# Attention in pairs of units with energies of 512 queries, and two turns moved from TensorE to DRAM blocks

## The chip, the cores and the metric

The kernel runs on one core of a Trainium2 chip. The metric is the device time of one execution in microseconds (us). Short names of the engines: PE is TensorE (its matrix multiplications; PEld its weight loads), DVE is VectorE, ACT is ScalarE, POOL is GpSimd, SP is SyncE, which here only issues transfers (DMAs).

## The reference, cut to what matters

The input `x` has shape (4, 64, 64, 256): four images of 4096 positions with 256 channels. Two layers follow each other.

```python
# layer 0: self-attention over the 4096 positions of an image
q, k, v = x @ wq + bq, x @ wk + bk, x @ wv + bv        # q, k: 32 channels, v: 256
attention = softmax(einsum('bnd,bmd->bnm', q, k))       # 4096 x 4096 per image
y = gamma * einsum('bnm,bmc->bnc', attention, v) + x
# layer 1: deformable convolution (16 groups, 3 x 3 points), then an MLP
h = ln(y) * ln1_g + ln1_b
p = h @ inproj_w                                         # the image that is sampled
t = gelu(ln(depthwise3x3(h)))                            # gives offsets and masks
offset, mask = t @ off_w, softmax(t @ mask_w)
z = y + (sum over points of mask * bilinear(p, point + offset)) @ outproj_w
out = z + gelu((ln(z) * ln2_g + ln2_b) @ fc1_w) @ fc2_w  # 256 -> 1024 -> 256
```

## The kernel before, in words

The work is cut into 64 units of 256 positions (16 per image; `NU` is 16, `UN` is 64). Each unit goes through the same stages, and the stages of neighbouring units overlap:

- `project` computes keys, queries and values. For the first image this is done at the start; for the others one unit at a time beside the attention of the image before. The later images read `x` by `in_blocks` (L70): four DMAs of 64 KB in pieces of 128 bytes that put every 32 x 32 block at its turned place, and one DVE `transpose` (L645) turns inside the blocks.
- `Attention` (the class at L696): for a unit, 32 tiles of 128 keys. `energies` makes 8 key tiles by 256 queries per step (L752, in a single-pass format, fp32r), into four PSUM tiles; `exponentials` lets ACT take the exponential (L762); `weighted` multiplies by the values (L774, plain f32, 257 columns: 256 channels and the row sum) into two accumulators. Every unit loads all keys again (`keys`, L713, two DMAs per 1024 keys).
- `front` scales by the reciprocal of the row sum (L797) and by gamma (L799), adds the input (L803), normalizes, turns on PE and projects (`pp`, L831) into the DRAM image `xp`.
- `plan` does the depthwise convolution on DVE (`cv`, L878), turns, normalizes, makes offsets and masks (`po`, L915), and builds the 5 x 5 weights `wn` of every position. `sums` (L961) and `mask` (L996) are issued once per tile of 128 positions, twice per unit.
- `sample` multiplies windows of 5 x 256 channels (`win`, loaded by two DMAs for each row pair, L1074) by `wn` and adds up, on DVE (`pw`, L1094 and L1102, 1280 elements each). The result `sp` goes to DRAM too (`spd`).
- `back` turns `sp` by four PE transposes (`pt_s`, L331), ACT copies it out of PSUM (L1169), `pout` (L1175) projects, `x1b` is added and normalized, `xn_b` is turned by four PE transposes (`pt_b`), ACT scales it (`hT_b`, L311), `ph` (L1200) and `pmlp` (L1217) are the MLP, and the result is written.

Every instruction of PE, DVE, ACT and POOL stands in an order written out by hand: `WHEN` gives each step of a stage a time in a slot of `T` = 60 (one unit), `LATE` has other times for the last units, and `whole` sorts all steps by these times. The times only order the steps; each engine runs its list in order and waits where something is not there yet. SP issues its DMAs in program order, and a DMA that waits holds up those behind it.

PSUM is full: two rotating tiles `m` for all small products, four tiles for the energies, two accumulators.

Of the kernel before, what the change touches and what calls it, by code (L numbers as in the profile page):

```python
# [20 lines left out]
def tile_attention_dcnv3_block(  # L21
# [126 lines left out]
    gamma_s = bcast(gamma, 1, "gamma_s")  # L148
# [118 lines left out]
    qd = dram.tile([UN, 2, CQ, 256], F32, name="qd")  # L267
# [9 lines left out]
    nc.vector.memset(most_, 1.0)  # L277

# [28 lines left out]
    def scaled(pt, g, b, name, m=256):  # L307

        hT = p3.tile([P, C // P, 256], F32, tag="cT", name=f"hT_{name}")
        for k in range(C // P):  # L310
            nc.scalar.activation(  # L311
                hT[:, k, :m], pt[:, k, :m], AF.Identity, bias=b[:, k : k + 1], scale=g[:, k : k + 1]
            )
        return hT
# [11 lines left out]
    def transposed(src, name, n=2, pool=None, tag="m"):  # L326

        pt = (pool or ps).tile([P, C // P, 256], F32, tag=tag, name=f"pt_{name}")
        for k in range(C // P):
            for i in range(n):  # L330
# [7 lines left out]
    T = 60.0  # L338
    WHEN = {
        "first": {  # L340
# [3 lines left out]
        "project": {  # L344
            "load": -14.4, "turn": 19.72, "copy": 23.24, "values": 37.05, "value_bias": 42.74, "keys": 48.45,
            "key_bias": 50.49,
        },
        "attention": {
            "load": -9.55, "e0": -5.06, "x0": -4.74, "e1": -0.37, "w0": 7.43, "w3": 19.94, "w2": 29.41,
            "x1": 34.36, "w1": 39.1, "w5": 39.21, "e2": 40.0, "w7": 40.03, "x2": 44.45, "w9": 44.91,  # L350
            "e3": 47.79, "w11": 48.15, "w8": 48.54, "w6": 48.74, "x3": 51.26, "w10": 52.64, "w14": 52.81,
            "w13": 56.88, "w4": 57.18, "w12": 58.34, "w15": 58.47,
        },
        "general": {
            "e0": -0.41, "x0": -0.39,
        },
        "tables": {
            "gelu0": -12.71, "gelu1": 13.84, "exp": 41.13,
        },
        "front": {  # L360
            "inverse": -0.5, "residual": -0.39, "stats": -0.12, "shift": 9.44, "norm": 19.11, "keep": 28.97,
            "turn": 29.19, "scale": 30.3, "project_in": 34.83, "image": 34.95, "store": 36.13,
        },
        "plan": {
            "tap0": 36.3, "tap1": 38.26, "tap2": 39.85, "tap3": 40.19, "tap4": 40.72, "tap5": 41.32,
            "tap6": 42.03, "tap7": 42.69, "tap8": 43.18, "turn": 45.14, "stats": 46.03, "shift": 47.25,
            "norm": 48.66, "turn2": 48.72, "gelu": 48.77, "heads0": 49.72, "bias0": 50.5, "heads1": 50.74,
            "bias1": 51.52, "mask_exp": 51.76, "hat0": 52.32, "sums": 52.79, "invert": 53.35, "hat2": 53.4,
            "hat1": 53.43, "weigh": 54.05, "nearer": 56.15, "near": 56.63, "bounds": 56.75, "mask0": 57.34,
            "mask1": 57.68, "product0": 58.16, "y_copies0": 58.81, "y0": 59.03, "product1": 59.29,  # L370
            "y1": 59.54, "y_copies1": 59.55, "carry": 60.61, "x_copies": 60.68, "x": 67.54, "count": 72.45,
        },
        "sample": {
            "rows01": 8.69, "times01": 8.71, "rows00": 19.04, "times00": 19.06, "rows02": 20.69,
            "times02": 20.71, "plus01": 21.46, "plus02": 30.61, "rows03": 31.73, "times03": 31.75,
            "rows04": 34.48, "times04": 34.5, "plus03": 34.93, "plus04": 38.23, "across00": 41.05,
            "across01": 43.53, "rows12": 45.24, "times12": 45.26, "across02": 45.73, "rows11": 45.98,
            "times11": 46.0, "rows10": 46.62, "times10": 46.64, "plus11": 47.22, "plus12": 47.46,
            "rows13": 48.74, "times13": 48.76, "rows14": 49.16, "times14": 49.18, "plus13": 50.33,
            "plus14": 51.1, "across10": 51.57, "across11": 51.74, "across12": 53.08,  # L380
        },
        "back": {
            "load": 18.32, "turn": 54.71, "copy": 54.86, "project_out": 56.05, "added": 58.14, "stats": 58.62,
            "shift": 59.05, "norm": 59.26, "raised": 59.37, "turn2": 59.4, "scale": 59.75, "hidden0": 59.78,
            "hidden5": 61.44, "gelu0": 65.24, "gelu5": 67.65, "hidden1": 68.95, "gelu1": 70.18,
            "hidden2": 73.18, "gelu2": 77.76, "hidden4": 81.06, "gelu4": 84.59, "hidden6": 84.61,
            "hidden7": 87.12, "gelu6": 87.36, "gelu7": 93.93, "hidden3": 99.62, "gelu3": 101.35,
            "narrowed0": 102.2, "narrowed1": 106.29, "end": 106.65,
        },
        "far": {  # L390
            "pair": -84, "point": -80, "left": -77, "rows": -76, "pixels": -74, "summed": -66, "turn": 46.75,
            "copy": 47.03, "project_out": 47.31, "added": 47.59, "stats": 47.87, "shift": 48.15,
            "norm": 48.43, "turn2": 48.72, "scale": 49.0, "raised": 49.28, "hidden0": 49.56, "gelu0": 49.84,
            "hidden1": 50.12, "gelu1": 50.4, "hidden2": 50.68, "gelu2": 50.96, "hidden3": 51.24,
            "gelu3": 51.52, "hidden4": 51.8, "gelu4": 52.08, "hidden5": 52.36, "gelu5": 52.65,
            "hidden6": 52.93, "gelu6": 53.21, "hidden7": 53.49, "gelu7": 53.77, "narrowed0": 54.05,
            "end": 54.33,
        },
        "checks": {
            "range": 14.0, "left": 14.1, "largest": 14.2,  # L400
        },
        "summing": {
            "rows01": 8.69, "times01": 8.71, "rows02": 12.39, "times02": 12.41, "pair01": 16.11,
            "sum01": 19.82, "rows03": 23.5, "times03": 23.52, "rows00": 27.2, "times00": 27.22,
            "sum00": 30.92, "rows04": 34.6, "times04": 34.62, "pair03": 38.33, "sum03": 42.03,
            "rows11": 45.24, "times11": 45.26, "summed0": 45.73, "rows12": 46.02, "times12": 46.04,
            "pair11": 46.82, "sum11": 47.61, "rows13": 48.37, "times13": 48.39, "rows10": 49.15,
            "times10": 49.17, "sum10": 49.95, "rows14": 50.71, "times14": 50.73, "pair13": 51.52,
            "sum13": 52.3, "summed1": 53.08,
# [5 lines left out]
        "attention": {  # L415
            60: {"e2": 41.63, "w7": 60.7, "x2": 61.55, "e3": 66.3, "w11": 68.16, "w10": 72.05, "x3": 77.04,
                "w4": 92.63, "w12": 96.73, "w14": 126.44, "w13": 147.54, "w6": 149.16, "w9": 151.58,
                "w8": 162.58, "w15": 163.18},
            61: {"load": 73.15, "e0": 77.73, "x0": 99.75, "e1": 104.68, "w0": 119.31, "x1": 120.96,
                "w4": 128.82, "w7": 135.45, "e2": 139.75, "w5": 140.73, "x2": 142.59, "w6": 144.13,  # L420
                "w9": 144.35, "e3": 145.78, "w11": 147.04, "w10": 148.04, "x3": 148.67, "w3": 150.79,
                "w13": 152.23, "w14": 153.3, "w2": 155.04, "w1": 159.09, "w12": 159.2, "w8": 161.6,
                "w15": 162.84},
            62: {"load": 99.58, "e0": 109.75, "x0": 110.1, "e1": 115.56, "w0": 118.27, "w2": 120.32,
                "x1": 120.74, "w6": 125.15, "e2": 126.82, "w5": 128.98, "x2": 130.87, "w7": 131.07,
                "e3": 132.81, "w11": 137.28, "w10": 140.15, "w1": 141.18, "x3": 141.21, "w3": 142.52,
                "w14": 145.25, "w4": 147.03, "w13": 147.58, "w12": 147.88, "w8": 148.09, "w9": 149.05,
                "w15": 151.71},
            63: {"load": 96.28, "e0": 109.66, "x0": 111.02, "w0": 116.5, "w1": 120.49, "e1": 121.69,
                "x1": 130.68, "w4": 132.65, "w5": 134.09, "e2": 139.76, "w2": 143.15, "w3": 145.56,  # L430
                "w6": 148.75, "x2": 149.1, "w10": 151.15, "e3": 151.17, "w7": 152.54, "w8": 159.2,
                "x3": 160.16, "w14": 161.32, "w12": 166.1, "w9": 172.0, "w13": 173.2, "w11": 173.78,
                "w15": 178.59},
        },
        "plan": {
            60: {"tap3": 42.14, "tap4": 45.5, "tap5": 45.93, "tap6": 48.85, "tap7": 56.79, "tap8": 69.29,
                "turn": 71.67, "stats": 84.78, "shift": 119.53, "norm": 125.14, "turn2": 134.12,
                "gelu": 136.3, "heads0": 139.79, "heads1": 139.85, "bias0": 140.11, "bias1": 141.55,
                "hat0": 143.63, "hat2": 145.22, "mask_exp": 149.39, "hat1": 152.25, "sums": 155.5,
# [170 lines left out]
                "summed0": 541.21},  # L610
        },
        "checks": {
            66: {"range": 530.02, "left": 563.34, "largest": 1080.93},
        },
    }

# [921 lines left out]
```

## Time and profile before

| | |
|---|---|
| time, median of 3 runs | 3755.57 us (3753.74 to 3757.58) |
| the profiled execution: time, span | 3755.45 us, 3753.7 us |
| PE busy | 3693.6 us (98%) |
| DVE busy | 3442.1 us (92%) |
| ACT busy, with 380 loads of a function table of 1283 ns | 2122.0 us (57%) |
| DMA, mean busy share of the 16 engines of queue q1 | 51.9%, 508 MB |
| mean granted PE clock | 0.995 |

The span reaches from the first instruction to the last; the other 1.75 us of the profiled execution lie around it. Busy time counts an engine once where its instructions overlap. Since they do overlap on PE and DVE, the mean duration of an instruction is longer than the distance between the starts of two in a dense row; this distance is called the pitch below, and sums of work are made with it. A page line of part 5 has the line, engine, operation, output and inputs, shape and count, then busy time and mean duration, then the idle time ahead of the group and what ended it.

### The profile page before, as it was taken

The page shows a single profiled execution, that of the slowest core. Times are in us where ns is not written, and L with a number is a line of the kernel's source. Part 1 is how long each engine was busy: PE and PEld are TensorE (multiplying, and loading weights), DVE is VectorE, ACT ScalarE, POOL GpSimd, SP SyncE. Part 2 cuts the span into 40 slices and gives each one's busy share as a digit, 9 for nine tenths or more (in the row PEclk, how much of TensorE's full clock was granted, in tenths as well). Part 3 has the DMA queues.
Part 4 walks back from the last instruction along what each step waited for, and adds up shares of the span by engine and source line. Part 5 has one row for each costly group of instructions (what it writes and reads, how often), then busy time and mean ns, then how long its engine had stood idle before and what let it go on. Part 6 is the DMA issues. An engine that isn't in the chain of part 4 may idle for free.

```text
span 3753.7 us, 53218 instructions
## 1 busy us (share of the span) xinstructions
PE 3693.6 (98%) x18226; PEld 3185.1 (85%) x18226; DVE 3442.1 (92%) x6307; ACT 2122.0 (57%) x4085; POOL 313.1 (8%) x444
## 2 busy tenths in 40 slices
PE   7999999999999999999999999999999999999988
PEld 6888888888888888888888888888888888888867
DVE  2499999999999999999999999999999999999995
ACT  2465565565565565565565555555565665565543
POOL 1000000000000000000000000000000000000021
PEclk9999999999999999999999999999999999999999
DMA  6555545556555555555656455555565545544531
GB/s 185 142 130 140 143 129 140 141 129 175 149 149 146 138 131 143 134 135 143 176 137 164 129 138 142 129 139 140 138 174 146 136 124 136 132 129 126 135 83 52
DMA packets 370088, 518.42 MB, mean 138 GB/s; under 512 B 144560, under 2 KB 287472, under 8 KB 369808
## 3 DMA queue, kind: packets, MB, share of 16 engines
q1 hardware_dynamic: 359904, 508.02, 51.9%
q10 hardware_dynamic: 8320, 3.43, 0.4%
q8 instruction: 147, 2.41, 0.3%
q0 software_dynamic: 1584, 3.47, 0.3%
q14 instruction: 133, 1.09, 0.1%
HBM read 385.91 MB, written 128.85 MB: 137 GB/s over the span
## 4 chain that ended last, share of the span: by engine, by line
PE 89%; DVE 5%; issue 0%; DMA 0%; ACT 0%; POOL 0%; DVEq 0%; SPq 0%; ACTq 0%; POOLq 0%
PE acc L774 43%; PE pmlp L1217 11%; PE ph L1200 11%; PE e L752 6%; PE po L915 5%; PE pout L1175 3%; PE pp L831 3%; PE pv L670 2%; DVE pw L1094 1%; PE pkq L651 1%; DVE cv L878 1%; DVE pw L1102 1%; PE pt_s L331 1%; PE pt_b L331 1%; PE pt_p L331 1%; PE pc L891 1%
## 5 line engine op out<-in xcount | busy, mean ns | idle before, releaser
L774 PE MATMUL acc<-V,ex 128*128 128x257 f32 x8192 | 1887.0, 380 | 0.0
L774 PEld LDWEIGHTS acc<-V,ex 128*128 128x128 f32 x8192 | 1537.3, 190 | 223.3 <-issue 21.7
L1094 DVE TENSOR_TENSOR pw<-win,wn 128x1280 f32<-128x1280 f32 x640 | 931.5, 1481 | 10.9 <-ACT wn L1038 1.9
L1102 DVE TENSOR_TENSOR pw<-pw,pw 128x1280 f32<-128x1280 f32 x492 | 729.7, 1483 | 0.1
L762 ACT ACTIVATE ex<-e 128x512 f32<-128x512 f32 x1024 | 529.7, 605 | 26.1 <-PE e L752 18.0
L1200 PE MATMUL ph<-hT_b,f1w 128*128 128x256 f32 (+1 forms) x2080 | 487.9, 377 | 5.2 <-ACT gT L1208 2.8
L1217 PE MATMUL pmlp<-f2w,gT 128*128 128x256 f32 x2048 | 462.7, 379 | 1.3 <-DVE x1b L1182 1.1
L1200 PEld LDWEIGHTS ph<-hT_b,f1w 128*128 128x128 f32 x2080 | 378.1, 190 | 67.3 <-ACT gT L1208 6.3
L1217 PEld LDWEIGHTS pmlp<-f2w,gT 128*128 128x128 f32 x2048 | 384.2, 190 | 51.8 <-DVE x1b L1182 1.4
L878 DVE SCALAR_TENSOR_TENSOR cv<-hs,dw,cv 128x256 f32<-128x256 f32 (+1 forms) x1076 | 424.3, 459 | 1.4 <-ACT cv L874 1.3
L303 ACT ACTIVATE xn_p<-pc,nm_p,rstd_p 128x256 f32<-128x256 f32 x128 | 65.4, 561 | 541.1 <-DVE nm_p L295 541.1
L1208 ACT ACTIVATE gT<-ph,f1b 128x256 f32<-128x256 f32 (+1 forms) x520 | 236.6, 468 | 236.1 <-PE ph L1200 234.6
L752 PE MATMUL e<-qs,kT 128*128 128x256 f32 x2048 | 321.7, 300 | 0.0
L752 PEld LDWEIGHTS e<-qs,kT 128*128 128x128 f32 x2048 | 271.4, 190 | 8.1 <-ACT ex L762 0.8
L762 ACT ACT_TABLE_LOAD x182 | 233.5, 1283 | 3.1
L289 POOL TENSOR_SCALAR rstd_p<-mv_p 128x2 f32<-128x2 f32 (+1 forms) x65 | 76.2, 1172 | 1669.1 <-DVE mv_p L287 1597.9
L915 PE MATMUL po<-om_w,ge 128*128 128x432 f32 x512 | 196.5, 526 | 0.8 <-ACT ge L908 0.8
L1004 DVE TENSOR_TENSOR pr<-hat 128x1296 f32<-128x1296 f32 x128 | 192.6, 1505 | 0.0
L1208 ACT ACT_TABLE_LOAD x124 | 159.1, 1283 | 2.2
L915 PEld LDWEIGHTS po<-om_w,ge 128*128 128x128 f32 x512 | 96.9, 190 | 70.5 <-issue 54.7
L908 ACT ACTIVATE ge<-pt_p,bd,gd 128x256 f32<-128x256 f32 (+1 forms) x130 | 66.0, 558 | 137.9 <-PE pt_p L331 137.9
L303 ACT ACTIVATE xn_b<-x1b,nm_b,rstd_b 128x256 f32<-128x256 f32 x128 | 70.0, 593 | 129.8 <-DVE nm_b L295 129.8
(220 smaller groups left out, 3823.0 us busy)
## 6 DMA issues: line engine op xcount, KB each, us to landing
win<-xp SPq DMA_DIRECT2D x536, 320.0 KB, 4.5
kT<-kd SPq DMA_DIRECT2D x512, 256.0 KB, 4.2
omd<-om SPq DMA_DIRECT2D x63, 432.0 KB, 2.6
x<-in_x_dram SPq DMA_DIRECT2D x64, 256.0 KB, 3.0
x1d<-x SPq DMA_DIRECT2D x64, 256.0 KB, 2.2
xp<-xq SPq DMA_DIRECT2D x128, 128.0 KB, 2.4
x1b<-x1d SPq DMA_DIRECT2D x63, 256.0 KB, 3.2
spd<-sp SPq DMA_DIRECT2D x63, 256.0 KB, 2.2
```

Of the source, the lines that this page charges most:

```text
L303: nc.scalar.activation(xn[:, i, :], s, AF.Identity, bias=nm[:, i : i + 1], scale=st["r"][:, i : i + 1])
L752: nc.tensor.matmul(es[r][:, jj, :], lhsT=self.kT[g][:, 4 * jj + r, :], rhs=self.qs.bitcast(F32R), start=True, stop=not self.general,)
L762: nc.scalar.activation(ex, self.es[r], AF.Exp)
L774: nc.tensor.matmul(self.acc[i], lhsT=ex[:, jj, i * P : (i + 1) * P], rhs=V[t // 2][:, t % 2, :], start=(g == 0 and r == 0 and jj == 0), st ...
L878: nc.vector.scalar_tensor_tensor(dst, src, dw[:, k, j : j + 1], dst, ALU.mult, ALU.add)
L915: nc.tensor.matmul(st["po", i], lhsT=st["ge"][:, k, i * P : (i + 1) * P], rhs=om_w[:, k, :], start=(k == 0), stop=(k == 1),)
L1004: nc.vector.tensor_mul(pr.rearrange("p a b c d g -> p a b (c d g)"), hat[:, :, i, 1, :].unsqueeze(1).to_broadcast([P, 3, 3, S]), hat[:, :, ...
L1094: nc.vector.tensor_mul(st[r].rearrange("p d (g c) -> p (d g) c", c=GC), src.rearrange("p d (g c) -> p (d g) c", c=GC), wns[v][:, i, r] .re ...
L1102: nc.vector.tensor_add(st[0], st[0], st[r])
L1200: nc.tensor.matmul(ph[:, :m], lhsT=f1w[:, k, c * P : (c + 1) * P], rhs=st["hT"][:, k, :m], start=(k == 0), stop=(k == 1),)
L1208: nc.scalar.activation(st["gT"][:, c, :m], st["ph", c][:, :m], AF.Gelu, bias=f1b[:, c : c + 1])
L1217: nc.tensor.matmul(po, lhsT=st["gT"][:, c, i * P : (i + 1) * P], rhs=f2w[:, c, :], start=(c == 0), stop=(c == NH - 1),)
```

## The change

The change has four parts.

1. Attention works on pairs of units. A slot is now a pair (`T` = 120). `energies(j)` makes 2 key tiles by 512 queries; 16 such steps per pair. It needs two PSUM tiles instead of four; each accumulator becomes a two-bank tile that holds both halves of one unit. `weighted(u, j)` is the same work as before, for one unit of the pair. The keys are loaded once per pair, by one DMA per 1024 keys, and the queries by two DMAs per pair. The last two units (62 and 63) run alone, with 256 queries, as before.
2. In `back` of units 1 to 58, `sp` and `xn_b` are not turned by PE. `sp` is read back from `spd` by `in_blocks` (four DMAs) and turned in its blocks by a DVE transpose into `sT`, so ACT's copy goes. `xn_b` is written to a small DRAM tile (`ways`), read back by four DMAs, turned by a DVE transpose (`swap`), and scaled by ACT in place. Both, and the input of `project`, use one tile, tag `xs`, of which there is one buffer.
3. DVE: gamma is multiplied into the value weights once, so L799 goes (128 instructions); one reciprocal per unit in place of two; `sums` and `mask` once per unit in place of twice.
4. `win` of a row pair is loaded by one DMA in place of two. All times of `WHEN` and `LATE` are new. By the new order ACT loads a function table 517 times (380 before), and SP issues 2136 DMAs (2454 before).

```diff
-    gamma_s = bcast(gamma, 1, "gamma_s")
+    gamma_s = bcast(gamma, 1, "gamma_s", True)
+    for t in (wv_s.rearrange("p k m -> p (k m)"), bv_s):
+        nc.vector.tensor_scalar(t, t, gamma_s, None, ALU.mult)
...
+    def blocks(name, src, t0=0):
+        t = p1.tile([P, C // P, 256], F32, tag="xs", name=f"bl_{name}")
+        in_blocks(t, src, t0, 2)
+        return t
+
+    def swapped(dst, bl):
+        nc.vector.transpose(dst.rearrange("p k t -> p (k t)"), bl.rearrange("p k t -> p (k t)"))
+        return dst
...
-    T = 60.0
+    T = 120.0
...
         def energies(self, j):
+            self.es = [ps_e.tile([P, 2, 256], F32, tag=f"e{r}", name=f"e_{self.n}_{j}_{r}") for r in range(2)]
+            for r in range(2):
+                if self.paired:
+                    whole = [(self.es[r], self.queries, 2 * j + r)]
...
+                for k, (e, q, t) in enumerate(whole):
+                    nc.tensor.matmul(
+                        e, lhsT=self.kT[t // 8][:, t % 8, :], rhs=q, start=True, stop=not self.general
+                    )
...
         def inverse():
-            for i in range(2):
-                nc.vector.reciprocal(rall[:, b * NU + u, i : i + 1], att.acc[i][:, C : C + 1])
-            for i in range(2):
-                nc.vector.tensor_mul(rg[:, i : i + 1], rall[:, b * NU + u, i : i + 1], gamma_s)
+            nc.vector.reciprocal(rall[:, b * NU + u, :], att.acc[u][:, :, C])
...
         def sums():
-            for i in range(nt):
-                nc.vector.tensor_reduce(
-                    ms[:, i, :], st["ml"][:, i].rearrange("p k g -> p g k"), AX.X, ALU.add
-                )
+            nc.vector.tensor_reduce(ms, st["ml"].rearrange("p i k g -> p i g k"), AX.X, ALU.add)
...
-        def mask(i):
-            hy = st["hat"][:, :, i, 1, :]
-            nc.vector.tensor_mul(hy, hy, st["mk"][:, i].unsqueeze(1).to_broadcast([P, 3, S]))
+        def mask():
+            hy = st["hat"][:, :, :, 1, :]
+            nc.vector.tensor_mul(hy, hy, st["mk"].unsqueeze(1).to_broadcast([P, 3, nt, S]))
...
         def turn():
-            st["pt"] = transposed(sp(), f"s_{name}", n)
+            if way is None:
+                st["pt"] = transposed(sp(), f"s_{name}", n)
+            else:
+                st["bl"] = blocks(f"s_{name}", spd, way * P)
 
         def copy():
...
+                swapped(st["sT"], st["bl"])
...
         def norm():
             normalised(st, parts(), f"b{name}")
+            if way is not None:
+                st["way"] = ways[(way + 1) // 2 % 2]
+                nc.sync.dma_start(st["way"].rearrange("(q p) c -> p q c", p=P), st["xn"])
...
         def turn2():
-            st["pt"] = transposed(st["xn"], f"b_{name}", n)
+            if way is None:
+                st["pt"] = transposed(st["xn"], f"b_{name}", n)
+            else:
+                st["bl"] = blocks(f"b_{name}", st["way"])
+
+        def swap():
+            st["hT"] = swapped(p3.tile([P, C // P, 256], F32, tag="cT", name=f"hT_b{name}"), st["bl"])
...
+            way=g0 if 0 < v < UN - 5 and not general else None,
```

The branch `general` is a fallback for inputs out of range; it does not run with these inputs.

## The prediction

> **What bounds the kernel now.** I read the busy times first, then the share of each engine in stretches of one unit, then who waited for whom, then the chain of work and the instructions in order of time.
>
> ```profile
> PE 3693.6 (98%) x18226; PEld 3185.1 (85%) x18226; DVE 3442.1 (92%) x6307; ACT 2122.0 (57%) x4085; POOL 313.1 (8%) x444
> ```
>
> ```profile
> 2000.00:2056.50 56.50, 56.50 (x282) 48.94 (x281) 53.79 (x97) 32.90 (x64) 4.40 (x6) 1.00 0.62 158
> ...
> 3000.00:3054.00 54.00, 54.00 (x270) 46.73 (x269) 52.31 (x94) 32.63 (x64) 4.40 (x6) 1.00 0.51 132
> ...
> 3700.00:3753.00 53.00, 40.99 (x215) 34.14 (x213) 20.41 (x41) 18.19 (x46) 1.88 (x3) 0.95 0.07 23
> ```
>
> The first is the page's line of busy times. In the second view the columns are the stretch, its length, then busy us of PE, PEld, DVE, ACT and POOL, clock, DMA share, GB/s. A unit of the first three images takes 56.5 us, one of the last image (which has no `project` beside it) 54.0 us. In both PE has no idle time. DVE is free for only 2.7 and 1.7 us.
>
> ```profile
> DVE x1b L1223 <- PE pmlp L1217: 5.1, 6, 0.9
> DVE om L924 <- PE po L915: 4.9, 7, 0.7
> DVE nm_b L295 <- POOL rstd_b L290: 4.2, 7, 0.6
> DVE rall L797 <- PE acc L774: 1.6, 7, 0.2
> DVE x1b L1182 <- PE pout L1175: 1.1, 7, 0.2
> ```
>
> These are all of DVE's waits between 1000 and 1400 us (total, times, longest). Three quarters are for PE, so they shrink when PE gets faster; the one for POOL does not. In the same stretch PE waited for nothing. So PE sets the pace, with DVE 5% behind it.
>
> **What the change takes from PE.** The chain of work gives PE's pitch (start, length, what):
>
> ```profile
> 2001.67 0.44 PE pt_s L331 x4
> 2002.10 0.95 PE e L752 x8
> 2003.06 1.73 PE pout L1175 x8
> ```
>
> A transpose costs 0.109 us, an energy matmul of 256 columns 0.119, a pass of 256 f32 columns 0.216.
>
> The 464 transposes that go (8 for each of 58 units) are 464 x 0.109 = 50.6 us.
>
> Energies: now 2048 x 0.119 = 243.2 us. After, 992 of 512 columns and 64 of 256. No row shows 512 columns. Above, twice 0.119 = 0.238: then nothing is saved. Below, the f32 passes: 432 columns (`po`, 2.90 us for 8 in the chain) against 256 give (0.3625 - 0.216) / 176 = 0.83 ns per column of an f32 pass; at half of that per column in the single-pass format, 512 columns cost 0.216. I take 0.216, since at 256 columns the load of the weights (mean 190 ns) can be what makes 0.119 out of a shorter stream. Sum 992 x 0.216 + 64 x 0.119 = 221.9, so 21 us saved (0 to 21). [...]
>
> PE saves 72 us (51 to 72): 0.34 + 0.87 = 1.21 us per unit, 55.3 in place of 56.5, and 52.8 in place of 54.0. Were PE alone to decide, with its other 91 us (3753.7 less 3663 of work at these pitches) as they are, the span would be 3682.
>
> **What it gives to DVE.** In order of time, columns as before:
>
> ```profile
> 2021.36 0.70 DVE L645 STREAM_TRANSPOSE xT<-xs 128x512 f32<-128x512 f32 x1
> 2021.99 0.65 DVE L824 TENSOR_TENSOR x<-x,ob 128x512 f32<-128x512 f32 x1
> ...
> 2011.84 0.28 DVE L799 TENSOR_TENSOR rg<-rall,gamma_s 128x1 f32<-128x1 f32 x2
> 2012.03 0.30 DVE L1021 TENSOR_TENSOR us<-pr 128x144 f32<-128x144 f32 x1
> ...
> 2000.29 0.70 DVE L961 TENSOR_REDUCE ms<-om 128x16 f32<-128x144 f32 x2
> 2000.91 0.41 DVE L1111 TENSOR_TENSOR sp<-pw 128x256 f32<-128x256 f32 x1
> ```
>
> A block transpose of the same size has a pitch of 0.63 us; two per unit add 1.26. Gone: two products by gamma, 0.19; one of two reciprocals, 0.09; of the two `sums` (0.62) about 0.16, since a merged one costs one pitch of 0.31 and 144 more elements at 1.04 ns (the slope between the 256- and 1280-element operations, pitch 0.33 and 1.40); of the two `mask` products (1.12 us together) 0.07 in the same way. Net +0.75 us per unit, and over the kernel 58 x 1.26 - 64 x 0.51 = +40 us. Scaling the value weights is about 1 us, once, at the start. DVE: 54.5 us per unit beside `project`, 53.1 in the last image.
>
> So PE (55.3) stays ahead in three images by 0.8 us per unit, and in the last image DVE (53.1 against 52.8) is the bound. This eats a fourth of the gain and more where PE and DVE wait for each other.
>
> **The ends.** The first reciprocal now runs at 117.2 us. At the pitches above, PE's list holds 82.6 us of work ahead of it before (16 projections of 3.03 us, unit 0's 128 passes of 0.217, its energies, 2.6 of the next image) and 105 us after, because most of unit 1's products stand between unit 0's. So DVE's steady work starts 22 us later, near 140, after some 28 us of early work as now: 111 idle. Until the second pair's results PE has 78 us of work and DVE 47; until the third 89 and 86: 34 idle. At the end DVE is idle now for 9.4 (3600 to 3700) and 33 us after 3700, which the last unit's chain through all engines makes; I keep 43. DVE's sum: 3442 + 41 + 111 + 34 + 43 = 3671. To it come its waits in between: where PE is the bound 0.8 us for each of some 42 units, 34; in the last image 0.4 for each of 11 (the POOL wait of 0.6 shrinks: the new order has 1.4 to 2.0 us of other work between the statistics and their use, against a gap of 1.45 that POOL needs), 4; and 6 for the turned tiles. Together 3715.
>
> **The turned tiles.** `sp` is written (2.2 us to landing), then four DMAs are issued (0.63 each) and land (2.6): 7.7 us with the issue of the write. In the new DVE order 8.6 to 10.8 us of other DVE work stand between the last add of `sp` and its transpose, so it fits with 1 to 3 us to spare; I take 0.1 us of wait on the mean. Behind the waiting transpose on DVE stand the taps of `plan` and the windows, and PE's `pout`. For `xn_b`: two ACT operations of 0.59, then the same way, 9 us, against 12 to 16. If the cover goes, each us of delay is up to 58 us.
>
> On SP, the block loads wait for the `xs` buffer and for the written data, and `win`, `kT` and the `xp` writes are queued behind. They have 5 us and more to spare where I followed them; SP itself issues fewer DMAs than before.
>
> [...] The row first: `xs<-in_x_dram`, 128-byte pieces, 64 KB, lands 2.6 us after its issue, 256 KB in 1 KB pieces (`x`) after 3.0. [...] Bandwidth: the share is 0.55 with `project` (1000 to 1400) and 0.48 without, so one such load is at most 0.07; two, less half of the key loads, leave it below 0.7.
>
> **ACT and POOL.** ACT loses 0.59 us per unit (the copy of `sT`) and gains 137 table loads of 1.283 us, 2.7 per unit: 35.0 of 55.3 us, hidden beside PE as long as exponentials stand ahead of their products; in the stretch where they alternate with GELU, two loads and two exponentials (3.8 us) stand against 4.3 us of PE work between the energies. POOL's work is the same.
>
> **The rivals.**
> - PE's whole gain arrives: 3682 to 3684. For it: PE never waits in the middle now. Against: DVE's sum above.
> - The turned tile is late by a few tenths, or 512 columns cost 0.238: 21 us less gain, 3738. For it: 1 to 3 us of cover, and one buffer. The second is also the way in which the pairs would do nothing.
> - Slower: DVE becomes the bound and keeps today's 2.7 us of waits. 54.5 + 2.7 = 57.2 per unit, +0.75 for 58 units and the later start: 3795. It decides from 2.0 us of waits per unit on (56.5 - 54.5). For it: both engines run their lists in order, and PE's `m` tiles wait for DVE. Against: three quarters of the waits are for a PE that gets faster.
>
> **How the numbers follow.** The likeliest, chance 0.47: span 3715, and with the 1.75 us around it 3717 (own range 3700 to 3730). The profiled execution took 3755.45, the median is 3755.57, so the forecast holds for the median too. The whole gain: 0.15. The half gain: 0.24, of which 0.10 lies above 3748. Slower: 0.14. A measurement of this kernel can tell about 0.2%, 7.5 us, from no change. Faster 0.47 + 0.15 + 0.14 = 0.76, same 0.10, slower 0.14. From 3680 to 3757 some 0.17 is left out, nearly all of it above.
>
> **What would show it.** Energies at 0.43 us for two; no `pt_s` and `pt_b` in the middle; a unit of 55.3 to 55.7 us with DVE busy 98% or more; the first reciprocal near 140; in the last image PE with idle time. The forecast is wrong if DVE waits for its blocks (`bl_s`, `bl_b`) by more than 0.5 us a unit, if PE waits for ACT's exponentials, or if the end gets longer than the 172 us that lie behind the last reciprocal now.

## The result and the profile after

The changed kernel takes 6603.94 us (median of 4, 6596.36 to 6605.33), the kernel before 3755.9 us beside it: 1.758 times as long, interval 1.755 to 1.761. The forecast was 3717.

The page of the kernel after, its busy times, the row of the DMA share in 40 slices, and the chain of work by engine and line:

```profile
PE 4063.4 (62%) x16770; PEld 3330.2 (50%) x16770; DVE 3512.5 (53%) x6107; ACT 2302.3 (35%) x4164; POOL 464.7 (7%) x444
...
DMA  3212222232222222223222222222222222222121
...
q1 hardware_dynamic: 580768, 488.58, 23.0%
...
DMA 47%; DVE 20%; SPq 19%; PE 9%; issue 2%; POOL 1%; ACT 1%; DVEq 0%; POOLq 0%; ACTq 0%
```

No engine of the core is busy for even two thirds of the time. PE, 89% of the chain before, is 9% of it; transfers and SP's queue are 66%. Yet the DMA engines are less busy than before, 23% against 51.9%, for as many bytes (488.6 MB on this queue). So transfers are waited for while most DMA engines stand still. The loads that were merged, with the write of `sp` beside them, on the pages before and after (count, KB each, median us from issue to landing, which the page after lacks):

```profile
win<-xp SPq DMA_DIRECT2D x536, 320.0 KB, 4.5
kT<-kd SPq DMA_DIRECT2D x512, 256.0 KB, 4.2
spd<-sp SPq DMA_DIRECT2D x63, 256.0 KB, 2.2
```

```profile
win<-xp SPq DMA_DIRECT2D x268, 640.0 KB
kT<-kd SPq DMA_DIRECT2D x132, 512.0 KB
```

Stretches of the kernel after (columns as before; the last two are DMA share and GB/s):

```profile
2000.00:2103.00 103.00, 64.08 (x269) 52.37 (x269) 58.65 (x98) 39.92 (x70) 5.82 (x5) 0.82 0.24 76
...
3015.00:3020.00 5.00, 0.00 (x0) 0.00 (x0) 0.00 (x0) 0.00 (x0) 0.00 (x0) 0.50 0.13 49
```

A unit takes some 103 us in place of 56. In the second stretch nothing computes for 5 us, and the DMA share is 0.13, as much as two engines of 16, at 49 GB/s. The chain (start, length, what) and SP's own order around that place:

```profile
3003.34 17.14 DMA ways<-xn_b
3020.48 0.02 issue
3020.49 1.58 SPq L76
```

```profile
2994.54 8.06 SPq L1617 DMA_DIRECT2D x1d<-x  x1
...
3003.34 5.96 SPq L1984 DMA_DIRECT2D ways<-xn_b  x1
3009.40 3.05 SPq L1500 DMA_DIRECT2D kT<-kd  x1
```

A write of 256 KB (`ways`) takes 17.1 us to land; `spd`, of the same size, took 2.2 before. Even the issue of a DMA takes SP 3 to 8 us in these rows, against about 0.6. What DVE waited for from 1000 to 1400 us:

```profile
DVE hT_b L291 <- DMA bl_b<-ways: 70.0, 4, 29.3
DVE sT L291 <- DMA bl_s<-spd: 34.4, 4, 11.7
DVE om L1716 <- PE po L1707: 25.0, 2, 12.6
DVE xT L1418 <- DMA xs<-in_x_dram: 24.0, 2, 12.1
```

The engines named are those that wait for the turned tiles. That makes the DRAM blocks look guilty; the next runs say otherwise.

### The profile page after: what moved, and what is told of

Its sections match the earlier page's. It is cut to its first block, busy times and chain, and to the rows that moved or that the text cites. A ratio compares the mean times of both kernels' runs of the same rounds, so it can differ in the third digit from the quotient of the medians.

```text
span 6603.5 us, 49623 instructions
## 1 busy us (share of the span) xinstructions
PE 4063.4 (62%) x16770; PEld 3330.2 (50%) x16770; DVE 3512.5 (53%) x6107; ACT 2302.3 (35%) x4164; POOL 464.7 (7%) x444
## 4 chain that ended last, share of the span: by engine, by line
DMA 47%; DVE 20%; SPq 19%; PE 9%; issue 2%; POOL 1%; ACT 1%; DVEq 0%; POOLq 0%; ACTq 0%
DMA ways<-xn_b 15%; SPq L76 12%; DMA spd<-sp 8%; DMA win<-xp 7%; DVE pw L1887 5%; DMA vd<-vs 4%; SPq L1486 4%; DVE pw L1879 4%; PE acc L1565 4%; DMA bl_b<-ways 4%; DMA x1d<-x 4%; DVE cv L1670 2%; DMA bl_s<-spd 2%; PE pout L1971 1%; DMA kT<-kd 1%
## 5 line engine op out<-in xcount | busy, mean ns | idle before, releaser
L1565 PE MATMUL acc<-V,ex 128*128 128x257 f32 x8192 | 2030.0, 400 | 23.9 <-ACT ex L1554 23.9
L1565 PEld LDWEIGHTS acc<-V,ex 128*128 128x128 f32 x8192 | 1656.8, 204 | 315.4 <-ACT ex L1554 25.7
L2006 PE MATMUL ph<-hT_b,f1w 128*128 128x256 f32 (+1 forms) x2080 | 584.4, 424 | 611.0 <-DVE xq L1630 401.7
L2006 PEld LDWEIGHTS ph<-hT_b,f1w 128*128 128x128 f32 x2080 | 427.7, 214 | 718.5 <-DVE xq L1630 410.6
L347 PE MATMUL pt_p<-ident,xn_p 128*128 128x128 f32 x256 | 67.1, 406 | 972.7 <-ACT xn_p L318 971.8
L291 DVE STREAM_TRANSPOSE hT_b<-bl_b 128x512 f32<-128x512 f32 x58 | 41.2, 710 | 957.8 <-DMA bl_b<-ways 957.8
L1971 PE MATMUL pout<-ow,sT 128*128 128x256 f32 x512 | 199.0, 557 | 539.8 <-DVE sT L291 527.9
L1544 PE MATMUL e<-qs,kT 128*128 128x512 f32 (+1 forms) x1056 | 444.6, 507 | 95.5 <-DMA kT<-kd 75.9
L1971 PEld LDWEIGHTS pout<-ow,sT 128*128 128x128 f32 x512 | 138.7, 283 | 589.8 <-issue 509.8
L291 DVE STREAM_TRANSPOSE sT<-bl_s 128x512 f32<-128x512 f32 x58 | 41.3, 711 | 709.7 <-DMA bl_s<-spd 709.7
L1716 DVE TENSOR_TENSOR om<-po,om_b 128x432 f32<-128x432 f32 x128 | 76.4, 601 | 442.5 <-PE po L1707 416.9
L304 POOL TENSOR_SCALAR rstd_b<-mv_b 128x2 f32<-128x2 f32 (+1 forms) x65 | 59.7, 919 | 3288.8 <-DVE mv_b L302 3154.8
```

The source lines that it names most:

```text
L1544: nc.tensor.matmul(e, lhsT=self.kT[t // 8][:, t % 8, :], rhs=q, start=True, stop=not self.general)
L1565: nc.tensor.matmul(self.acc[u][:, i, :], lhsT=ex[:, i * P : (i + 1) * P], rhs=V[j][:, jj, :], start=(t == 0), stop=(t == NT - 1),)
L1971: nc.tensor.matmul(po[:, i, :], lhsT=st["sT"][:, k, i * P : (i + 1) * P], rhs=ow[:, k, :], start=(k == 0), stop=(k == 1),)
L2006: nc.tensor.matmul(ph[:, :m], lhsT=f1w[:, k, c * P : (c + 1) * P], rhs=st["hT"][:, k, :m], start=(k == 0), stop=(k == 1),)
```

## The experiments

### Which transfers: the loads taken apart

Part of the change is that each window and each key group is loaded by one DMA, and the queries of a pair by two, where half by half they take four. The source of each such DMA has two rows on the outside (two image rows, or a step of zero for the second copy):

```diff
-            for r in range(2):
-                row0 = xp[b, y + 2 + r, 0:1, :]
-                nc.sync.dma_start(t[r * W : (r + 1) * W]..., bass.AP(xp.tensor, row0.offset, [[C, W], [1, WIN * C]]))
+            nc.sync.dma_start(t..., bass.AP(xp.tensor, row0.offset, [[WP * C, 2], [C, W], [1, WIN * C]]))
```

The first run puts the halves back everywhere, two more for one kind only, and one merges the windows in the kernel before.

> The kernel after, but each window, each key group and the queries are again loaded half by half (two, two and four DMAs in place of one, one and two), so that the slowest dimension of every source is 32 or 64 and not 2. Theory A (a source with two rows on the outside keeps the whole DMA on 2 of the 16 engines, and everything on SP's queue stands behind it): the time goes back to what the prediction worked out for the rest of the change, 3700 to 3750 us; the DMA share in the steady part rises from 0.12 to about 0.6, the write of xn_b lands in about 2.5 us in place of 13 to 17. Theory B (the turns through DRAM blocks are the cause: 128-byte pieces, a round trip, one buffer): nothing that matters changes, over 6000 us.

> The kernel after with only the windows loaded half by half; keys and queries stay merged. Theory A: 132 key loads of 512 KB and 64 query loads of 128 KB still run at about 50 GB/s, 10.5 and 2.6 us each, about 24 us per unit of 55 in which two engines are taken; each delays what is queued behind it by up to 10 us, so slower than the first run by a few per cent up to a third: 3800 to 5000 us. Theory B: over 6000 us.

> The kernel after with only keys and queries loaded half by half; the windows stay merged. Theory A: 268 loads of 640 KB at 50 GB/s are 13 us each, 3500 us in all, on two engines on which the other traffic has its share too (about 330 MB over 16 engines, 1/8 of it at 25 GB/s an engine: some 800 us on each of the two): about 4300 us if that queue never pauses, 4300 to 5500. Theory B: over 6000 us.

> The kernel before with one edit: each window is loaded by one DMA of 640 KB whose source has two rows on the outside, in place of two of 320 KB. Theory A: as in the run with only the windows merged, 13 us per window on two engines, 4.2 windows per unit: 4300 to 5500 us, though nothing is turned through DRAM more than before. Theory B: the time of before, 3756 us within 1%.

> Keys and queries half by half as in the first run; each window in two DMAs of 320 KB, the size and number of before, but cut by columns, so that both still have two rows on the outside of the source. Theory A (the two outer rows, not the size): as with the windows merged, 5485 us within 5%, each DMA near 6.5 us at 50 GB/s. Rival (one DMA of 640 KB is simply too long): back to about 3791 us.

Measured, in order: 3790.8 us (1.0096 of before, 1.0080 to 1.0113); 4707.9; 5485.3; 5083.9; 5562.6 (the last four are one execution each). In the fourth nothing is turned through DRAM that was not before, and one edit of a load costs 1329 us. In the last one the DMAs have the size and number of before, and it stays slow. So it is the two outer rows: not the blocks, and not the size. The first run's page has a share of DMA near that of before (49.3% on queue q1, 51.9% before), and landing times like those of before:

```profile
DMA  5454555455555454546555545455645544545431
...
win<-xp SPq DMA_DIRECT2D x536, 320.0 KB, 4.2
kT<-kd SPq DMA_DIRECT2D x264, 256.0 KB, 3.7
```

The sizes fit. In the trace a packet of 5120 bytes (one partition's row of a window) takes 0.205 us in the kernel after, and 0.310 in the first run, so the packets themselves did not become slow; 128 of them on two engines are 13.1 us per window, 3516 us for 268. Keys (16,896 packets at 0.165) and queries (4096 at 0.087) add 1575, and a sixteenth of all other packets, taken as spread evenly over the 16 engines, is 920: 6010 us of work for each of the two engines, 91% of the 6603 us span. Reckoned in the same way the two engines are busy for 4897 of 5082 us with the windows merged in the kernel before, 4797 of 5484 in the third run, 4976 of 5561 in the last. In the second it is 3355 of 4706, only 71%; the waits of what stands behind the two engines make the rest, as far as this reckoning goes.

The packets show it too. In the kernel after, two window packets are under way at once for 93.5% of the time in which any is; in the kernel before it is 14 to 17 for 62% of that time. The share of 0.13, these packets and the five runs agree on two engines for two outer rows. Other sizes than 2 were not tried, and what spreads a DMA over the engines is not shown.

With its loads apart the kernel has 2600 DMAs on SP, more than before the change (2454), and is quick. This leaves 74 us between 3791 and the forecast.

### Which engine sets the pace without the merged loads

The first run's pairs of units take 112.3 us in the middle (110.6 forecast), with three of 117 to 119 and two of 114.7 at the ends of images. There value loads (L1466), which wait for PE, stand between the block loads on SP; SP's program order, as the rows show, is not the order of the steps:

```profile
846.28 1.28 SPq L76 DMA_DIRECT2D bl_s<-spd  x2
850.04 0.58 SPq L1466 DMA_DIRECT2D V<-vd  x1
850.67 1.28 SPq L76 DMA_DIRECT2D bl_s<-spd  x2
```

Three runs tried that and the balance of PE and DVE. One gives SP the order of the steps; two turn `sp` by PE again:

```diff
+ engines={..., nc.sync.engine}             # sp_steps: SP follows the steps too
- st["bl"] = blocks(..., spd, way * P)      # sp_pe, sp_pe_last: four PE transposes
+ st["pt"] = transposed(sp(), ...)          # and nc.scalar.copy in place of DVE's transpose
```

> The first run (all loads half by half) with SP's DMAs put in the order of the hand-written steps as well. There the value loads of the next image, which wait for PE to give the old values free, stand between the four block loads of one tile at three places, and the pairs of units there take 117 to 119 us in place of 112.3. Theory E (that is what makes them long): the long pairs go, about 20 us, to 3771 us. Rival (the blocks are late there because of the traffic, or PE is late for another reason): 3791 us. What could spoil it: in step order the windows are asked for only just ahead of their use; then it gets slower than 3791 with DVE waiting for windows.

> The first run with sp turned again by PE (four transposes) and copied by ACT in units 3 to 58; xn_b still goes through DRAM. Theory P (PE sets the pace of the first three images, DVE that of the last): 44 units x 4 x 0.109 us are 19 us more, the 12 of the last image save 0.63 us of DVE each, 8 us, and the waits for bl_s at the ends of the images, some 5 us, go: about 3797 us. Rival D (DVE sets the pace throughout): 56 x 0.63 us less, 3756 us.

> The first run with sp turned by PE and copied by ACT only in units 47 to 58, those of the last image. Theory P: DVE paces the last image, 12 x 0.63 us less, 3783 us. Rival (PE paces it too): 12 x 0.44 us more, 3796 us.

Measured: 4165.2 us (1.108), 3821.4 (1.0170), 3804.9 (1.0125). In the first the windows are asked for too late (DVE waits for `win` for 33 us of 400), so it says nothing on the blocks. In the second the long pairs are gone (114.3 against 113.6 us for the others), but all other pairs are at least 1.1 us longer, where eight transposes cost 0.87: PE now waits for ACT's copy ahead of `pout` (3.0 us from 2900 to 3300 us in the third run). Both runs are slower than either theory had it, and with that wait in them they don't tell which engine was the bound.

Three more edits, and the last two together:

```diff
- nc.tensor.matmul(e, lhsT=kT, rhs=q)                        # e256: two of 256 columns
+ for h in range(2): nc.tensor.matmul(e[:, h], lhsT=kT, rhs=q[:, h])
- "hidden0": 190.4673, "gelu0": 192.3364                     # gelu_tog: beside hidden7, gelu7
+ "hidden0": 194.5694, "gelu0": 196.4386
+ sp turned by PE if v % 16 in (9, 10, 11, 12) and v < 47    # edges_pe; best has this and gelu_tog
```

> The first run with each energy matmul of 512 queries made as two of 256 into the same PSUM tile (four per step in place of two; all else, the pairs included, stays). Theory S (in steps of two, the 512-column matmul costs 0.235 us net, what two of 256 columns cost before, so the wide form saves nothing): 3791 us within 8, at most one more load of weights per step. The prediction's term (0.216 against 0.119): 992 x 0.022 = 22 us more, 3813 us.

> The first run with one GELU of ACT (hidden0 and gelu0 of the first unit of a pair) moved to stand beside the next GELU, so that its own two loads of a function table go. Theory G (three table loads around one exponential make PE wait 0.7 us in every pair): the pairs fall from 112.3 to about 111.6, over 28 pairs 15 to 20 us: 3773 us, with some 25 to 30 loads of each kind fewer. Rival (DVE, 97% busy, takes the place of PE at once): 3788 to 3791 us.

> The first run with sp turned by PE only in the four units at each end of an image at which value loads stand between the block loads (units 9 to 12, 25 to 28 and 41 to 44). Theory E (bl_s is late there because the value loads ahead of it on SP wait for PE): the three pairs of 117 to 119 us fall to about 114, 12 x 4 x 0.109 = 5 us of transposes are included: 3777 us. Rival (those pairs are long for another reason): 3791 to 3796 us.

> The two edits before this one together. By both theories 15 to 20 and 14 us off 3791: about 3759 us, level with the kernel before, and the rest of the loss is the start (23 us) and the end (12 us). If DVE takes over as the bound: about 3775 us.

Measured: 3791.5, 3793.7, 3797.6 and 3793.4 us (1.0100 to 1.0112): none gains. In the third the long pairs fall to some 114 us, and the pairs beside them rise from 112.3 to between 114 and 115.5. The first compares the widths directly. The order of time of PE in the first run, in this one, and in the kernel before (start, busy time, what; the next row's start shows how long the step holds PE, and the last row of each view is cut off by the end of its stretch):

```profile
1242.08 0.81 PE L1544 MATMUL e<-qs,kT 128*128 128x512 f32 x2
1242.73 1.46 PE L1565 MATMUL acc<-V,ex 128*128 128x257 f32 x6
```

```profile
1242.73 0.82 PE L1546 MATMUL e<-qs,kT 128*128 128x256 f32 x4
1243.39 0.81 PE L1567 MATMUL acc<-V,ex 128*128 128x257 f32 x3
```

```profile
1072.06 1.30 PE L752 MATMUL e<-qs,kT 128*128 128x256 f32 x8
1073.19 1.03 PE L774 MATMUL acc<-V,ex 128*128 128x257 f32 x4
```

Two of 512 columns hold PE for 0.65 us, four of 256 for 0.66, eight of 256 for 1.13. About 0.18 us of each is time in which the pass before still ends: the eight f32 passes ahead of such a step read 1.55 us, where eight at 0.216 are 1.73. So 512 columns cost 0.235 us net, two of 256 in the old steps 0.238: the wide form saves 0.1 us per pair, not 0.68.

In the second of these runs PE's waits for GELU (0.5 us in two pairs of the first run) are gone without any gain, which pointed at DVE. In the first run it was busy 109.4 us of a pair, and waited only for POOL (first run, 1222 to 1446 us, two pairs):

```profile
DVE nm_b L310 <- POOL rstd_b L305: 3.0, 4, 0.9
DVE nm_p L310 <- POOL rstd_p L305: 1.2, 2, 0.6
```

109.4 + 2.1 is 111.5 of 112.3 us. The next runs take these waits away, by moving what waits:

```diff
- "stats": 159.8131, "shift": 162.4299, "norm": 162.8037    # back of the first unit
+ "stats": 159.8131, "shift": 163.5, "norm": 163.52         # behind one more product of DVE
- "shift": 48.0374, "norm": 49.1589                         # plan of the first unit
+ "shift": 50.3, "norm": 50.35
- "stats": 217.0093, "shift": 219.2523                      # back of the second unit
+ "stats": 217.0093, "shift": 219.7                         # behind the statistics of plan
```

> The first run with three operations of DVE (nm_b of both units of a pair, nm_p of the first), each moved behind the next one or two operations of DVE in its order, so that POOL has time for the reciprocal roots; nothing is added or removed. Theory D (DVE is the bound of the steady part: 109.4 us busy per pair plus 2.1 us in which it waits for POOL, whose operations take up to 1.9 us beside products of 1280 elements): the pair falls from 112.3 by 0.5 to 2.1 us, to where PE (which is then the bound) stands: over 28 pairs 14 to 50 us, 3741 to 3777 us. Theory P (PE is the bound at 112 us): 3791 us, no change.

> The run before this one with the GELU moved as well. If DVE was the first bound and PE with its GELU waits (0.7 us a pair) the second, this takes the pair down by up to 0.7 us more, to about 111: 3735 to 3760 us. If PE's own work is 112 us or DVE's 112 us whatever the waits, it adds nothing to the run before this one.

> The run before this one with sp turned by PE in the twelve units at the ends of images. Where the block loads stand behind value loads, three pairs are 5 to 6 us longer than the others; PE's transposes put 5 us in: 0 to 10 us less than the run before this one, since alone the edit gained nothing.

Measured: 3757.1 us (1.0005, 0.9996 to 1.0014), 3757.2, and 3754.3 (0.9996, 0.9987 to 1.0005). Three operations of 0.16 us each, put one or two places later, are worth 34 us. DVE with its waits was the bound. The stretch of two pairs in the run with the loads apart, and in the first of these three:

```profile
1222.00:1446.00 224.00, 223.25 (x1024) 188.32 (x1023) 218.21 (x373) 140.18 (x257) 28.07 (x24) 1.00 0.51 132
```

```profile
1222.00:1446.00 224.00, 224.00 (x1033) 190.55 (x1032) 221.55 (x379) 142.74 (x257) 28.49 (x24) 1.00 0.51 133
```

DVE is 99% busy now, and the 16 pairs away from the ends take 110.7 us on the mean. PE reads 99.7% and 100% busy, and yet finishes 1033 matmuls where it had finished 1024: most of what it lost to DVE stood in the profile as busy time (only 0.75 us of the first stretch are idle), so a full PE was no proof that PE was the bound. The GELU adds nothing here either. In the last of the three DVE waits 8.2 us for `bl_b` between 640 and 990 us, where in the first it waits 7.4 for `bl_s`: to cure one of two blocked loads moves the wait to the other. So turning `sp` on PE there gained only 3 us.

### The value loads off SP's queue

```diff
-        nc.sync.dma_start(V[u][:, :, :C], vd[u])
+        nc.gpsimd.dma_start(V[u][:, :, :C], vd[u])     # v_scalar: nc.scalar
```

> The run with the three operations of DVE and the GELU moved, and now the value loads of the next image issued by POOL in place of SP, so that no block load stands behind one. At the ends of the images two pairs are 8 and 2 us longer than the others; three times that is 30 us. Theory E (they are long because the block loads, for sp or, with sp on PE, for xn_b, stand on SP behind value loads that wait for PE): up to 30 us less, 3727 to 3740 us. Against it: POOL waits for PE too then, and the roots that DVE needs stand behind it; then the pairs stay as long, 3750 to 3760 us.

> The same with the value loads issued by ACT. Theory E: 3727 to 3740 us, if ACT, busy 63% of a pair, can stand the waits for PE; if exponentials come late behind them, PE waits: 3745 to 3770 us.

> The run with the value loads on POOL (3741 us), and sp turned by PE and copied by ACT in units 3 to 58 as in the earlier run of that kind. There DVE with its waits for POOL was the bound. Theory F (with those waits gone PE is the bound of the first three images, as forecast): 44 units x 4 x 0.109 us = 19 us more there, less the 10 us in which DVE still waits for bl_s at the ends of images, and up to 6 us more in the last image: 3750 to 3760 us. If DVE is still the bound, its 56 x 0.63 us less give 3706 to 3730 us.

Measured: 3741.2 us (0.9960, 0.9946 to 0.9974), 3791.5 (1.0093), 3795.5 (1.0104). With the loads on POOL the long pairs fall from 118.1, 119.1 and 118.7 (the run with the GELU moved as well) to 112.8, 112.6 and 112.4, so the value loads on SP's queue were their cause; from 640 to 990 us DVE's waits for blocks fall from 8.9 to 3.3 us. On ACT exponentials and taps stand behind the waiting loads (from 740 to 1000 us PE waits 5.0 us for `ex`, DVE 6.1 for a tap), and those pairs grow to 127 and 128. The first is 15 us (0.4%) faster than the kernel before: the change with its loads apart, three operations of DVE and a GELU in other places, and 48 loads on another queue.

The last asked what turning `sp` through DRAM is worth once DVE is free of POOL. Pairs are 113.2 us in place of 110.9; the whole is 54 us longer, not 9 to 19. Neither theory had that. Of the 2.4 us per pair eight transposes are 0.87. The rest shows as new waits: of PE for ACT's copy (0.7 us per pair) and of DVE for `bl_b` (2.4 us per pair, none before). The one step drew the others out of their places, so this run doesn't price it by itself.

### Where the time stands

From the starts of the reciprocals of units 0, 48 and 63 in the order of time, in us:

| | to unit 0 | 0 to 48 | 48 to 63 | behind | span |
|---|---|---|---|---|---|
| before | 117.2 | 2682.3 | 781.4 | 172.8 | 3753.7 |
| loads apart | 140.7 | 2663.9 | 799.8 | 184.6 | 3789.0 |
| and three operations later | 142.0 | 2633.5 | 793.7 | 184.0 | 3753.2 |
| and GELU moved, value loads on POOL | 141.6 | 2619.7 | 795.9 | 182.1 | 3739.4 |

The forecast had 140 and 172 us for the ends, and so 3403 between; the last row has 3415.6 there. Of the 24 us that its span is above the forecast's 3715, 10 lie behind the last reciprocal and 13 between, where units 48 to 63 take 14.5 us more than before. The traces place 12.7 of these in the step from unit 62 to unit 63, which run alone after the change: 66.8 us in place of 54.1, with DVE 98% busy and 124 instructions of DVE in place of 105. More of DVE's work stands there; no run moved it.

## Why the prediction was wrong

**The step that failed** is the one on SP and bandwidth: "SP itself issues fewer DMAs than before", with "5 us and more to spare" for what is queued. The merged loads were costed at nothing; the part counts DMAs and bytes, and never the engines that a DMA runs on. What the runs show in its place: each merged load takes two engines (13.1 us per window, 6010 us of work for each of the two in all), and whatever stands behind it waits. Loaded half by half again, the kernel takes 3791 us, so 2813 of its 6604 come from there. The forecast even read the DMA share as a limit (below 0.7) and took for granted that a transfer can use all of it. Below 0.7 was right for the kernel with its loads apart (0.48 to 0.57 in stretches of 400 us), and no use for one in which half of all bytes (253 of 499 MB) go through an eighth of the engines.

Its other steps can be judged by the runs with the loads apart:

- **What the change takes from PE.** The transposes are gone from the middle. The energies were the wrong end of a stated pair of bounds: 0.216 taken, 0.235 measured, against 0.238 as the upper bound. The 21 us are about 3. The half per column behind the 0.216 was the author's assumption, and no row stood for it: by the 0.119 and the 0.235 a column costs 0.45 ns ((0.235 - 0.119) / 256, an estimate), against the 0.83 of an f32 pass.
- **DVE's sum** of 54.5 us per unit was right: 109.4 us busy per pair, against 109.0. In the last image, with DVE's waits gone, pairs take 107.1 us with PE idle for some 1 us, as the forecast's 53.1 and 0.4 of waits had it.
- **DVE's waits** were wrong in one term. The forecast let the wait for POOL shrink, since 1.4 to 2.0 us of other work stood against "a gap of 1.45 that POOL needs". It grew from 0.6 to 1.05 us per unit, since POOL's time is not fixed. In the kernel before and in the first run (start, length, what; first POOL's rows, then DVE's beside them):

```profile
1104.29 0.33 POOL L289 TENSOR_SCALAR rstd_b<-mv_b 128x2 f32<-128x2 f32 x1 [20.07 <-DVE mv_b L287]
1104.70 0.84 POOL L290 TENSOR_TENSOR rstd_b<-rstd_b,minus_half 128x2 f32<-128x2 f32 x1
...
1104.68 0.30 DVE L1024 TENSOR_TENSOR us<-us,pr 128x144 f32<-128x144 f32 x1
1105.57 0.16 DVE L295 SCALAR_TENSOR_TENSOR nm_b<-mv_b,rstd_b 128x2 f32<-128x2 f32 x1 [0.60 <-POOL rstd_b L290]
```

```profile
1318.29 1.29 POOL L304 TENSOR_SCALAR rstd_b<-mv_b 128x2 f32<-128x2 f32 x1 [42.65 <-DVE mv_b L302]
1319.67 0.71 POOL L305 TENSOR_TENSOR rstd_b<-rstd_b,minus_half 128x2 f32<-128x2 f32 x1
1321.62 1.31 POOL L304 TENSOR_SCALAR rstd_p<-mv_p 128x2 f32<-128x2 f32 x1 [1.25 <-DVE mv_p L302]
1323.01 1.81 POOL L305 TENSOR_TENSOR rstd_p<-rstd_p,minus_half 128x2 f32<-128x2 f32 x1
...
1318.05 1.46 DVE L1880 TENSOR_TENSOR pw<-win,wn 128x1280 f32<-128x1280 f32 x1
1320.41 0.16 DVE L310 SCALAR_TENSOR_TENSOR nm_b<-mv_b,rstd_b 128x2 f32<-128x2 f32 x1 [0.90 <-POOL rstd_b L305]
```

  The same two operations take 1.25 us beside products of 144 elements and 2.1 to 3.2 beside those of 1280. Putting DVE's operations behind the next ones took 34 us off.
- **The rival "DVE becomes the bound"** named the right engine, but that its 3795 lies near the 3791 measured is luck. It priced a unit at 57.2 us, above the 56.5 of before; a pair of 112.3 is 56.15 a unit. Its own terms with the later start of 22 us make 3821, not 3795. By the table, the 35 us that the run with the loads apart has more than before are 23.5 at the start, 11.8 at the end and 18.4 in units 48 to 63, less 18.4 gained in units 0 to 48.
- **The turned tiles.** The cover of 8.6 to 10.8 us held in the middle: no wait for blocks in the two pairs shown. The block loads land in 2.5 us, as the row had it. At the ends of the images it failed. The forecast named what is queued behind the block loads, and not the value loads that stand among them. Taking those off SP is worth 16 us (3757.2 less 3741.2).
- **The ends.** The first reciprocal at 140.7 was right (near 140). The 172 us behind the last became 184.6.
- **PE's 110.6 us per pair** were met once DVE's waits were gone (110.7 on the mean), though not by the same terms: the energies save 0.6 us less than forecast, and what makes up for it the runs don't show.

Of the signs that would have made the forecast wrong, DVE's waits for its blocks (957.8 and 709.7 us over 58 units) showed the failure at once. They name who waits, though, and not why.

## What to carry to other kernels

Before two DMAs are merged into one, look at the outermost dimension of the source's access pattern: here a 2 there kept a load on two engines of 16 (a share of 0.13), and everything that was queued behind on the two paid. A low DMA share (23% on queue q1) together with long landings (17.1 us for 256 KB) was the sign of it; the tiles that are waited for need not belong to the transfer at fault. When two engines are both as busy as PE and DVE here (99.7% and 97% in the first run), look at each small wait of either and at what runs beside it, for here three operations of 0.16 us in another place were worth 34 us.

## What the runs showed of the hardware

- POOL's operations of two elements per partition take 0.2 to 1.9 us. In the kernel before 63 of 380 take more than 1 us, in the first run 210, nearly all of them beside DVE products of some 1280 elements; 126 of the 210 end within 0.1 us of a DVE operation's end. What makes them longer there, no run separated.
- PE's granted clock fell to 0.50 after a short wait. In the first run PE waits 1.56 us for `xn_p` at 2967.65, and soon after the clock is at half for 3.4 us:

```profile
2967.00:2969.00 2.00, 0.65 (x3) 0.19 (x1) 1.40 (x4) 0.41 (x1) 1.36 (x1) 1.00 0.56 90
...
2971.00:2972.00 1.00, 1.00 (x4) 0.81 (x3) 1.00 (x2) 1.00 (x3) 0.00 (x0) 0.50 0.00 0
```

  This costs some 1.7 us more (an estimate, half of 3.4): the wait is doubled. Waits of 1.98, 2.03 and 1.55 us in the same run (at 1791, 2696 and 2856 us) were not followed by such a stretch, so the length of a wait alone does not decide; what does, these runs don't show. In the kernel after 168 stretches are at half clock, 2538 us together, and its mean clock is 0.808. PE is busy for 4063 us there against 3694 before, with less work; but PE is only 9% of the chain.
- With the merged loads SP's queue is held up too: 342 of its 2136 issues take more than 3 us, where none takes more than 2.2 in the kernel before and in the first run. The reason is not shown.
